# Paged attention behind a conditional mix, one core: the mixed tile is transposed by VectorE and transfers instead of TensorE, the opening is reordered and the last projection is cut into two column halves

## The chip, the cores and the metric

One core of a Trainium2 chip runs the whole program. The time is the device time of one execution in microseconds (us). Three executions of the kernel before took 2167.09, 2168.49 and 2169.05 us, so the median is 2168.49 us. Lower is better. All arithmetic is float32.

## What is computed

The input x has 64 batches of 32 tokens with 512 channels. It goes through two residual layers:

```python
# layer 1: each batch mixes its 32 tokens with one of 16 matrices
W = weights[condition]                       # 64 x 32 x 32
x = x + einsum('bct,bcd->bdt', x, W)
# layer 2: attention over 512 cached tokens (16 pages of 32) and the 32 new ones
q = rope(rmsnorm(x @ Wq.T)); k = rope(rmsnorm(x @ Wk.T)); v = x @ Wv.T   # 32 q heads, 8 k/v heads, D = 128
k_all = concat(k_cache[block_table], k); v_all = concat(v_cache[block_table], v)
p = softmax(where(valid, q @ k_all.T / sqrt(128), -1e30))
x = x + (p @ v_all) @ Wo.T
```

## The kernel before

**Tiles and steps.** The 64 batches make 16 tiles of 4 batches (128 tokens, one per partition). The 8 key heads are split into two halves of 4. The loop over steps (L949) runs first all 16 tiles with half 0, then all 16 with half 1: 32 steps. In a step the loops over 4 batches (`bt`) and 4 key heads (`g`) make 16 slots, numbered 0 to 15.

**One slot.** `scores` (L591) makes the scores of one batch and head on TensorE (`ps`), and ScalarE takes their exponential (`pr`). `values` (L647) multiplies the `pr` of the slot before with the cached values (`po`), and VectorE adds and divides. `head_keys` (L582) copies the keys of one head of the next batch out of the raw pages `k_t` into `kh` on VectorE.

**Pieces between slots.** The step also prepares the next ones. For the step after it (`ahead`, n+1): the key projection `k_a` in slot 3, the four query projections `q_a` in slots 4 to 7, and the value projection `v_a` in slot 13. All of these take the transposed tile `x1t` as weights (`project`, L420). The output projection of the step before, `out_proj` (L534), lies in slots 8 and 9. For the step after next (`beyond`, n+2) the residual tile `acc` is loaded in slot 11 (`x1_a`, L359), the mix is made in slot 14 (`x1_c`, L371: one TensorE product `pmix` with a block-diagonal matrix `bd`, then a VectorE addition), and the transposed tile is made in slot 15 (`x1_b`, L378: four TensorE transposes into `px1t`, a ScalarE copy to `x1t`, L385, and a store of `x1t` to device memory, L387 and L390, which ScalarE's queue issues). In the second half of the heads nothing is mixed: `x1_t` (L365) loads the stored `x1t` in slot 13.

**What sets the order.** TensorE and SyncE (SP) run in the order in which the program is written (L88); VectorE, ScalarE and GpSimd are ordered by a scheduler, except in the opening (L90), where all five are written out by hand. SP issues nearly all transfers, one after the other: the 16 pages of keys of each batch (L306; the pages of a batch are issued two batches ahead of its scores, and those of the batch prepared in slot 12 as 8 pages in slot 12 and 8 in slot 13, L957 and L998), the spreading of the query rows (L487), the loads and stores of `acc` (L363, L554). Transfers issued by SP and ScalarE share eight completion semaphores in turn: each transfer waits, before it is issued, until the transfer eight before it has landed. The raw pages have two buffers, `x1t` and the working tiles `w1` and `w2` one each, `acc` three.

**The opening.** The first tile's `acc` is loaded and mixed (L815) and transposed (L823) with short filler products (`keep_warm`, L803) around it. VectorE computes the rotation angles of the first two tiles (`positions`, `angles`, L819 to 821) before the transpose is asked for; ScalarE has the sines of the first angles ahead of the copy of the first `x1t`. ScalarE's queue issues the small inputs in the order condition, page table, lengths, frequencies (L747 to L793).

**The end.** After the last slot `out_proj` of the last step is done at once (L1047): 16 products of 128x512, one addition, one store. With 12 of them issued, `in_range` (L1035) lets TensorE sum a check on the denominators.

Of the kernel before, what the change touches and what calls it, by code (L numbers as in the profile page):

```python
# [55 lines left out]
def cond_resid_paged_attention_kernel(  # L56
# [69 lines left out]
    def positions():  # L126
        nc.vector.memset(half_pi, math.pi / 2)
        nc.vector.memset(minus_half, -0.5)
        nc.vector.tensor_copy(pos, lens_sb)
        nc.vector.tensor_scalar(pos, pos, row, None, ALU.add)  # L130
# [34 lines left out]
            scale=-1.0,  # L165
        )

    def cached_rows(pages_at, lens_at):

        row2 = const.tile([P, 1], F32, tag="row2", name="row2")  # L170
        nc.vector.tensor_scalar(row2, row, float(NHH), None, ALU.mult)
        nc.vector.tensor_scalar(
            v_row, pages_at, float(PSIZE * NHH), row2, ALU.mult, ALU.add
        )
        nc.vector.tensor_copy(lens_all, lens_at)
        for c in range(VC):
            key = const.tile([P, 1], F32, tag=f"key{c}", name=f"key{c}")
            nc.vector.tensor_scalar_add(key, part, float(c * P))
            nc.vector.tensor_scalar(valid[:, :, c], lens_all, key, None, ALU.is_gt)
# [15 lines left out]
    def steps_of(exact, pools):  # L195
# [130 lines left out]
        def fetch(n, c, **place):  # L326

            place = place or {"tag": "raw", "bufs": RAW}
            if c == 0 and n == NT * BT:
                other_half(1.0)  # L330
            b = n % (NT * BT)
            raw = work.tile([P, GH, D], F32, name=f"raw_{b}_{c}_{uid}", **place)
            nc.gpsimd.indirect_dma_start(  # L333
                out=raw.rearrange("p g d -> p (g d)"),
                out_offset=None,
                in_=vc,
                in_offset=bass.IndirectOffsetOnAxis(
                    ap=v_row[:, b * VC + c : b * VC + c + 1], axis=0
                ),
            )  # L340
            raws[n, c] = raw
# [22 lines left out]

        def x1_t(st):  # L365

            if st.hh:
                st.x1t = work.tile([P, KC, P], F32, tag="x1t", name=f"x1t_{st.name}", bufs=1)
                nc.sync.dma_start(st.x1t.rearrange("p c q -> p (c q)"), x1t_d[st.t])

        def x1_c(st):  # L371
            if st.hh:
                return
            pm = ps_p.tile([P, 512], F32, tag="pp", name=f"pmix_{st.name}")
            nc.tensor.matmul(pm, bd, st.acc, start=True, stop=True)  # L375
            nc.vector.tensor_tensor(st.acc, pm, st.acc, ALU.add)

        def x1_b(st):  # L378
            if st.hh:
                return  # L380
            pm = ps_p.tile([P, KC, P], F32, tag="pp", name=f"px1t_{st.name}")
            for c in range(KC):
                nc.tensor.transpose(pm[:, c, :], st.acc[:, c * P : (c + 1) * P], ident)  # L383
            st.x1t = work.tile([P, KC, P], F32, tag="x1t", name=f"x1t_{st.name}", bufs=1)
            nc.scalar.copy(st.x1t, pm)  # L385
            if st.n or exact:
                keep_x1t(st, nc.scalar)  # L387

        def keep_x1t(st, eng):
            eng.dma_start(x1t_d[st.t], st.x1t.rearrange("p c q -> p (c q)"))  # L390

        def rot_tables(st):

# [98 lines left out]
        def by_tensor(st):  # L492
            return st.n < 2 or exact
# [16 lines left out]
        def k_a(st):  # L510
            name = f"k_{st.name}"
            finish(st, GH, project(st, wt["k", st.hh, 0], f"pp_{name}"), name, "k")
# [18 lines left out]
        def q_b(st, g):  # L531
            to_columns(st, g)

        def out_proj(st, part, halfway=None):  # L534

            if part.start == 0:
                st.po = ps_p.tile([P, HID], F32, tag="pp", name=f"pout_{st.name}")
            for i in range(part.start, part.stop):
                if halfway and i == 3 * QH // 4:
                    halfway()  # L540
                nc.tensor.matmul(  # L541
                    st.po,
                    st.ot[:, i, :],
                    wt["o", st.hh, i // 4][:, i % 4, :],
                    start=(i == 0),
                    stop=(i == QH - 1),
                )
            if part.stop == QH:
                nc.vector.tensor_tensor(st.acc, st.po, st.acc, ALU.add)  # L549
                if exact or st is steps[-1]:  # L550
                    store(st)

        def store(st):
            nc.sync.dma_start(  # L554
                out[st.t * P : (st.t + 1) * P, :] if st.hh else acc_d[st.t], st.acc
            )

        def new_ot(st):
            st.ot = act.tile([P, QH, P], F32, tag="ot", name=f"ot_{st.name}", bufs=1)
# [185 lines left out]
        steps = [Step(n) for n in range(NHH * NT)]  # L745
        if not exact:
            nc.scalar.dma_start(cond_row, cond.rearrange("(i s) t -> s t i", s=S)[0:1])  # L747
            nc.scalar.dma_start(pages_sb, pages)
            nc.gpsimd.dma_start(norm_w["q"], qn_w.partition_broadcast(P))
            nc.gpsimd.dma_start(norm_w["k"], kn_w.partition_broadcast(P))  # L750
        if exact:
            nc.gpsimd.memset(vn_bufs[0], 0.0)
            nc.gpsimd.memset(vn_bufs[1], 0.0)
            key_no = wpool.tile([P, LK], F32, tag="key_no", name="key_no")
            key_no_i = work.tile([P, LK], I32, tag="sm", name="key_no_i")
            nc.gpsimd.iota(key_no_i, pattern=[[1, LK]], base=0, channel_multiplier=0)
            nc.vector.tensor_copy(key_no, key_no_i)
            nc.vector.memset(key_no[:, L:LK], -1e9)
            for st in steps:
                if st.t == 0:  # L760
                    load_w("k", st.hh)
                    load_w("v", st.hh)
                    for g in range(GH):
                        load_w("q", st.hh, g)
                        load_w("o", st.hh, g)
                if not st.hh:
                    load_cond_weights(st.t)
                x1_a(st)
                x1_t(st)
                x1_c(st)  # L770
                x1_b(st)
                rot_tables(st)
                k_a(st)
                k_b(st)
                v_a(st)
                for g in range(GH):
                    q_a(st, g)
                    q_b(st, g)
                new_ot(st)
                for bt in range(BT):  # L780
                    exact_batch(Batch(st, bt), key_no)
                out_proj(st, slice(0, QH))
            return
# [5 lines left out]
        nc.sync.dma_start(w_all, w_cond.rearrange("(n s) e -> s n e", s=S))  # L789
        load_w("q", 0, 0)  # L790
        load_w("q", 0, 1)
        nc.scalar.dma_start(lens_sb, lens)
        nc.scalar.dma_start(freq, inv_freq.partition_broadcast(P))  # L793
        load_w("k", 0, eng=nc.gpsimd)
        pages_at = work.tile([P, B * VC], I32, tag="pr", name="pages_at", bufs=3)
        nc.scalar.dma_start(pages_at, pages_v)
# [6 lines left out]
        def keep_warm(n):  # L803
            warm = ps_p.tile([P, P], F32, tag="pp", name="warm")
            for _ in range(n):
                nc.tensor.matmul(warm, ident, ident, start=True, stop=True)
# [9 lines left out]
        load_cond_weights(1)  # L816
        load_w("q", 0, 3)
        later = Batch(first, 1)
        positions()  # L819
        trig = work.tile([P, 3, TRIG * HD], F32, tag="w1", name="trig0", bufs=1)  # L820
        angles(0, trig)
        keep_warm(4)
        x1_b(first)  # L823
        keep_warm(3)
        rot_tables(first)
        nc.vector.memset(vn_bufs[0][:, :, D : D + 1], 1.0)
        nc.vector.memset(vn_bufs[1][:, :, D : D + 1], 1.0)
        cached_rows(pages_at, lens_at)
        trig = work.tile([P, 3, TRIG * HD], F32, tag="w1", name="trig1", bufs=1)
        reduced(TRIG, trig)  # L830
        q_a(first, 0)
        sines(TRIG, trig)
        early = small.tile([P, 1], F32, tag="rs", name="early")
        nc.scalar.activation(early, half_pi, AF.Exp)
        fetch(0, 0)
        fetch(0, 1)
        k_a(first)
        fetch(0, 2)
        keep_x1t(first, nc.gpsimd)
        q_a(first, 1)  # L840
# [108 lines left out]
        for st in steps:  # L949
# [3 lines left out]
            for bt in range(0 if st.n else 1, BT):  # L953
                this, after = batch, None
                n = st.n * BT + bt + 2
                if n < NHH * NT * BT:
                    after = Batch(steps[n // BT], n % BT, NPP // 2 if bt == BT - 1 else NPP)  # L957
                    unfilled += [(after, c) for c in range(VC)]
                for g in range(GH):
                    slot = bt * GH + g  # L960
# [32 lines left out]
                        if slot == 11:  # L993
                            x1_a(beyond)
                    if slot == 13:
                        if beyond:
                            x1_t(beyond)
                        for load in after.pages_left if after else ():  # L998
                            load()
                    if slot == 14 and beyond:  # L1000
                        x1_c(beyond)
                    if slot == 15 and beyond:
                        x1_b(beyond)
                    if slot == 1 and st.n == NT:
                        count(0)
                    if st.n == 1 and slot in (4, 5):
# [37 lines left out]
                redo, pc, float(P * NHH * NT * BT * GH), None, ALU.not_equal  # L1044
            )

        out_proj(steps[-1], slice(0, QH), in_range)  # L1047

    redo = const.tile([1, 1], I32, tag="redo", name="redo")
    run(False)  # L1050
# [54 lines left out]
```

## Time and profile before

The profiled execution took 2168.11 us, and its span (first to last instruction) is 2166.3 us, so 1.8 us lie outside the span.

| engine | busy us | share of the span |
|---|---|---|
| TensorE (PE) | 2144.2 | 99% |
| TensorE weight load (PEld) | 1494.4 | 69% |
| VectorE (DVE) | 1196.5 | 55% |
| ScalarE (ACT) | 868.9 | 40% |
| GpSimd (POOL) | 804.7 | 37% |

| group | count | busy us | mean ns |
|---|---|---|---|
| `po`, PE | 4096 | 551.1 | 277 |
| `pp_q`, PE | 1024 | 463.2 | 595 |
| `pout`, PE | 1024 | 450.2 | 592 |
| `pmix`, PE | 32 | 16.5 | 597 |
| `px1t`, PE | 64 | 9.7 | 273 |
| `x1t` copy, ACT | 16 | 9.3 | 581 |

A product of two float32 tiles is recorded as two passes, a transpose as one. PE products overlap, so the mean duration of one is longer than what it adds to the engine's time; the busy time counts overlaps once. "Idle before, releaser" of a group is the time its engine stood still ahead of it, and what ended most of that. For SP the timeline shows when each transfer is issued, not when it lands; a landing is seen only where something waits for it.

### The profile page before, as it was taken

What the parts mean: (1) busy time and instruction counts of PE and PEld (TensorE: products, weight loads), DVE (VectorE), ACT (ScalarE), POOL (GpSimd) and SP (SyncE); (2) the same over time, 40 slices, a digit from 0 to 9 for tenths busy, and PEclk for the clock granted to TensorE, in tenths of its full rate; (3) what the DMA queues carried; (4) which work ended last, traced back from release to release, by engine and by line L of the source; (5) the groups of instructions that cost most, each with busy time, mean ns of one, the idle gap of its engine ahead of it and who ended that gap; (6) DMA issues with size and microseconds to landing.
All of it is one profiled execution on the core that took longest, in us unless ns stands there. A gap on an engine that the chain in (4) does not pass through costs nothing.

```text
span 2166.3 us, 41552 instructions
## 1 busy us (share of the span) xinstructions
PE 2144.2 (99%) x12972; PEld 1494.4 (69%) x12972; DVE 1196.5 (55%) x2883; ACT 868.9 (40%) x1577; POOL 804.7 (37%) x1005
## 2 busy tenths in 40 slices
PE   7999999999999999999999999999999999999998
PEld 4766777667776677766777766777666777667775
DVE  5666555666455564465554565644566545556442
ACT  3544444444333344333444333443334443334441
POOL 4433333433333343333433343433434333334330
PEclk9999999999999999999999999999999999999999
DMA  8765555555655556556766855565545565555551
GB/s 248 193 164 162 157 172 157 148 155 160 172 152 152 151 160 174 154 150 196 224 177 179 212 158 164 157 178 159 156 141 169 162 174 159 153 153 163 171 162 54
DMA packets 387638, 357.51 MB, mean 165 GB/s; under 512 B 55024, under 2 KB 317296, under 8 KB 387408
## 3 DMA queue, kind: packets, MB, share of 16 engines
q1 hardware_dynamic: 342864, 213.87, 35.1%
q0 software_dynamic: 41648, 136.74, 21.6%
q10 hardware_dynamic: 2896, 4.14, 0.5%
q8 instruction: 106, 1.74, 0.3%
q14 instruction: 124, 1.02, 0.2%
HBM read 302.64 MB, written 12.58 MB: 146 GB/s over the span
## 4 chain that ended last, share of the span: by engine, by line
PE 97%; ACT 0%; issue 0%; DVE 0%
PE po_x L653 22%; PE ps_x L595 21%; PE pout_x L541 20%; PE pp_q_x L423 20%; PE pp_k_x L423 5%; PE pp_v_x L423 5%; PE pnv_x L637 2%; PE psn_x L613 1%; PE pmix_x L375 1%; PE px1t_x L383 0%; PE pt_x L467 0%; ACT pr_x L603 0%; ACT v_x L346 0%; DVE acc_x L549 0%; ACT nv_x L645 0%
## 5 line engine op out<-in xcount | busy, mean ns | idle before, releaser
L333 POOL DMA_INDIRECT raw_x<-in_vc_dram,v_row x512 | 540.4, 1055 | 820.4 <-ACT v_x L346 752.0
L603 ACT ACTIVATE pr_x<-ps_x 128x512 f32<-128x512 f32 x512 | 305.9, 597 | 825.5 <-PE ps_x L595 756.8
L653 PEld LDWEIGHTS po_x<-v_x,pr_x 128*128 128x128 f32 x4096 | 515.7, 192 | 126.9 <-issue 114.5
L653 PE MATMUL po_x<-v_x,pr_x 128*128 128x129 f32 x4096 | 551.1, 277 | 2.3 <-ACT pr_x L603 1.6
L423 PE MATMUL pp_q_x<-wq_x,x1t_x 128*128 128x512 f32 x1024 | 463.2, 595 | 8.5 <-ACT x1t_x L385 8.2
L541 PE MATMUL pout_x<-wo_x,ot_x 128*128 128x512 f32 x1024 | 450.2, 592 | 0.0
L595 PE MATMUL ps_x<-q_cols_x,kh_x 128*128 128x128 f32 x3072 | 405.4, 275 | 0.0
L595 PEld LDWEIGHTS ps_x<-q_cols_x,kh_x 128*128 128x128 f32 x3072 | 376.1, 192 | 15.1 <-issue 14.6
L346 ACT ACTIVATE v_x<-raw_x,valid 128x512 f32<-128x512 f32 x512 | 363.0, 716 | 5.3 <-DMA raw_x<-in_vc_dram,v_row 5.1
L541 PEld LDWEIGHTS pout_x<-wo_x,ot_x 128*128 128x128 f32 x1024 | 189.7, 190 | 214.3 <-issue 214.0
L423 PEld LDWEIGHTS pp_q_x<-wq_x,x1t_x 128*128 128x128 f32 x1024 | 185.8, 191 | 194.4 <-issue 185.6
L588 DVE COPY kh_x<-k_t_x 128x512 f32<-128x512 f32 x506 | 206.0, 417 | 188.1 <-PE ps_x L595 153.8
L671 DVE TENSOR_TENSOR nv_x<-po_x,nv_x 128x258 f32<-128x258 f32 x256 | 108.4, 424 | 314.9 <-PE po_x L653 279.9
L440 POOL TENSOR_TENSOR rs_q_x<-ms_q_x,minus_half 128x4 f32<-128x4 f32 x128 | 140.8, 1100 | 170.1 <-DVE ms_q_x L438 169.9
L433 ACT ACTIVATE sq_q_x<-pp_q_x 128x512 f32<-128x512 f32 x128 | 76.6, 598 | 272.9 <-PE pp_q_x L423 178.9
L595 PE MATMUL ps_x<-q_last_x,kh_x 128*128 128x128 f32 x1024 | 135.2, 275 | 0.0
L549 DVE TENSOR_TENSOR acc_x<-pout_x,acc_x 128x512 f32<-128x512 f32 x32 | 22.1, 692 | 199.3 <-PE pout_x L541 199.3
L595 PEld LDWEIGHTS ps_x<-q_last_x,kh_x 128*128 128x128 f32 x1024 | 124.6, 192 | 0.0
L423 PE MATMUL pp_k_x<-wk_x,x1t_x 128*128 128x512 f32 x256 | 116.3, 597 | 0.9 <-ACT x1t_x L385 0.9
L423 PE MATMUL pp_v_x<-wv_x,x1t_x 128*128 128x512 f32 x256 | 115.2, 592 | 0.0
L674 DVE TENSOR_TENSOR o_x<-nv_x,rden 128x256 f32<-128x256 f32 x256 | 108.6, 424 | 6.2
L437 DVE TENSOR_REDUCE ms_q_x<-sq_q_x 128x4 f32<-128x512 f32 x128 | 86.5, 676 | 45.1 <-ACT sq_q_x L433 44.6
(105 smaller groups left out, 1455.1 us busy)
## 6 DMA issues: line engine op xcount, KB each, us to landing
k_t_x<-in_kt_dram SPq DMA_DIRECT2D x2048, 64.0 KB
q_cols_x<-rows_x SPq DMA_DIRECT2D x360, 80.0 KB
q_last_x<-rows_x SPq DMA_DIRECT2D x120, 80.0 KB
raw_x<-in_vc_dram,v_row POOLq DMA_INDIRECT x512
wo_x<-in_wo_dram SPq DMA_DIRECT2D x32, 256.0 KB
acc_x<-in_x_dram SPq DMA_DIRECT2D x16, 256.0 KB
acc_d<-acc_x SPq DMA_DIRECT2D x16, 256.0 KB
wq_x<-in_wq_dram SPq DMA_DIRECT2D x8, 512.0 KB
```

Source lines behind the costliest of these rows:

```text
L333: nc.gpsimd.indirect_dma_start(out=raw.rearrange("p g d -> p (g d)"), out_offset=None, in_=vc, in_offset=bass.IndirectOffsetOnAxis(ap=v_ro ...
L346: nc.scalar.activation(v_bufs[b % 2][:, c, :, 0:D], raw, AF.Copy, scale=ok)
L423: nc.tensor.matmul(pp, st.x1t[:, c, :], w[:, c, :], start=(c == 0), stop=(c == KC - 1))
L437: nc.vector.tensor_reduce(ms, sq, AX.X, ALU.add)
L440: nc.gpsimd.tensor_tensor(rs, ms, minus_half, ALU.pow)
L541: nc.tensor.matmul(st.po, st.ot[:, i, :], wt["o", st.hh, i // 4][:, i % 4, :], start=(i == 0), stop=(i == QH - 1),)
L588: last["dve"] = nc.vector.tensor_copy(k, ba.k_raw[:, :, g, :]).ins
L595: nc.tensor.matmul(ps[:, c, :], ba.k[g][:, c * P : (c + 1) * P], queries(ba, g), start=True, stop=True,)
L603: last["act"] = nc.scalar.activation(pr, ps, AF.Exp, scale=SCALE).ins
L653: nc.tensor.matmul(ba.po[:, g % 2, :], ba.pr[g][:, c, :], ba.v_t[:, c, g, :], start=(c == 0), stop=(c == VC - 1),)
L671: nc.vector.tensor_tensor(t, ba.po, t, ALU.add)
L674: nc.vector.tensor_tensor(ba.o[:, both, :], t[:, :, 0:D], rd.unsqueeze(2).to_broadcast([P, 2, D]), ALU.mult,)
```

## The change

1. `x1_b` takes a new way for the tiles of steps 2 to 15 (14 tiles), `x1_turn`. VectorE transposes the mixed tile in blocks of 32x32 into a `w1` tile, and SP issues four transfers, one per batch, that store the blocks in device memory at the places of the full transpose, in runs of 32 floats (128 bytes). TensorE's transposes, ScalarE's copy and ScalarE's store are gone for these tiles. The first two tiles keep them.
2. The mix (`x1_c`) and `x1_turn` both move to slot 13, behind `v_a` and ahead of the last 8 pages that slot 13 issues.
3. The stored tile is loaded into `x1t` (`x1_t`) at the beginning of the next step: after the first 4 of the 16 pages that are issued there (`back`), and the other 12 pages follow.
4. Opening: the first `x1t` is asked for ahead of the angles; ScalarE's copy goes ahead of the sines; frequencies and lengths are issued ahead of the page table; `cached_rows` is cut in two, the row numbers come after the first query projection and the masks (`looked_at`) after the first key projection.
5. The last projection is made in two halves of 256 columns, each with its own addition and store; the check on the denominators lies in the first.

```diff
         def x1_t(st):
-            if st.hh:
-                st.x1t = work.tile([P, KC, P], F32, tag="x1t", name=f"x1t_{st.name}", bufs=1)
-                nc.sync.dma_start(st.x1t.rearrange("p c q -> p (c q)"), x1t_d[st.t])
+            st.x1t = work.tile([P, KC, P], F32, tag="x1t", name=f"x1t_{st.name}", bufs=1)
+            nc.sync.dma_start(st.x1t.rearrange("p c q -> p (c q)"), x1t_d[st.t])
...
         def x1_b(st):
             if st.hh:
                 return
+            if not by_tensor(st):
+                return x1_turn(st)
...
+        def x1_turn(st):
+            turned = work.tile([P, KC * BT, S], F32, tag="w1", name=f"x1w_{st.name}", bufs=1)
+            nc.vector.transpose(turned, st.acc.rearrange("p (j d) -> p j d", d=S))
+            kept = x1t_d[st.t].rearrange("(j d) (c b x) -> b d c j x", d=S, b=BT, x=S)
+            for b in range(BT):
+                nc.sync.dma_start(
+                    kept[b],
+                    turned[b * S : (b + 1) * S, :, :].rearrange("p (c j) x -> p c j x", c=KC),
+                )
...
+                back = bt == 0 and ahead and not ahead.hh
                 if n < NHH * NT * BT:
-                    after = Batch(steps[n // BT], n % BT, NPP // 2 if bt == BT - 1 else NPP)
+                    after = Batch(
+                        steps[n // BT],
+                        n % BT,
+                        NPP // 4 if back else NPP // 2 if bt == BT - 1 else NPP,
+                    )
+                    if back:
+                        x1_t(ahead)
+                        for load in after.pages_left:
+                            load()
...
                     if slot == 13:
-                        if beyond:
+                        if beyond and beyond.hh:
                             x1_t(beyond)
+                        elif beyond:
+                            x1_c(beyond)
+                            x1_b(beyond)
                         for load in after.pages_left if after else ():
                             load()
-                    if slot == 14 and beyond:
-                        x1_c(beyond)
-                    if slot == 15 and beyond:
-                        x1_b(beyond)
...
+            nc.scalar.dma_start(freq, inv_freq.partition_broadcast(P))
+            nc.scalar.dma_start(lens_sb, lens)
             nc.scalar.dma_start(pages_sb, pages)
...
-        nc.scalar.dma_start(lens_sb, lens)
-        nc.scalar.dma_start(freq, inv_freq.partition_broadcast(P))
...
+        keep_warm(4)
+        x1_b(first)
+        keep_warm(3)
         positions()
         trig = work.tile([P, 3, TRIG * HD], F32, tag="w1", name="trig0", bufs=1)
         angles(0, trig)
-        keep_warm(4)
-        x1_b(first)
-        keep_warm(3)
         rot_tables(first)
...
-        cached_rows(pages_at, lens_at)
...
+        cached_rows(pages_at)
         fetch(0, 0)
         fetch(0, 1)
         k_a(first)
+        looked_at(lens_at)
...
-        out_proj(steps[-1], slice(0, QH), in_range)
+        out_proj(steps[-1], slice(0, QH), slice(0, HID // 2), in_range)
+        out_proj(steps[-1], slice(0, QH), slice(HID // 2, HID))
```

More of the change, by code (lines that the diff above doesn't have):

```diff
@@ L166, in sines, with cached_rows @@
         )
-    def cached_rows(pages_at, lens_at):
+    def cached_rows(pages_at):
         row2 = const.tile([P, 1], F32, tag="row2", name="row2")
@@ L174, in cached_rows, with looked_at @@
         )
+    def looked_at(lens_at):
         nc.vector.tensor_copy(lens_all, lens_at)
@@ L532, in q_b, with out_proj @@
             to_columns(st, g)
-        def out_proj(st, part, halfway=None):
-            if part.start == 0:
+        def out_proj(st, part, cols=slice(0, HID), halfway=None):
+            if part.start == 0 and cols.start == 0:
                 st.po = ps_p.tile([P, HID], F32, tag="pp", name=f"pout_{st.name}")
@@ L541, in out_proj @@
                 nc.tensor.matmul(
-                    st.po,
+                    st.po[:, cols],
                     st.ot[:, i, :],
-                    wt["o", st.hh, i // 4][:, i % 4, :],
+                    wt["o", st.hh, i // 4][:, i % 4, cols],
                     start=(i == 0),
@@ L548, in out_proj, with store @@
             if part.stop == QH:
-                nc.vector.tensor_tensor(st.acc, st.po, st.acc, ALU.add)
+                nc.vector.tensor_tensor(st.acc[:, cols], st.po[:, cols], st.acc[:, cols], ALU.add)
                 if exact or st is steps[-1]:
[L551 to L556, printed above, removed]
+                    store(st, cols)
+        def store(st, cols=slice(0, HID)):
+            dst = out[st.t * P : (st.t + 1) * P, :] if st.hh else acc_d[st.t]
+            nc.sync.dma_start(dst[:, cols], st.acc[:, cols])
         def new_ot(st):
@@ L768, in steps_of @@
                 x1_a(st)
-                x1_t(st)
+                if st.hh:
+                    x1_t(st)
                 x1_c(st)
```

## Prediction

> **What bounds the kernel now.** I read the page first, its busy times and its chain of work that ended last.
>
> ```profile
> PE 2144.2 (99%) x12972; PEld 1494.4 (69%) x12972; DVE 1196.5 (55%) x2883; ACT 868.9 (40%) x1577; POOL 804.7 (37%) x1005
> ...
> PE 97%; ACT 0%; issue 0%; DVE 0%
> ```
>
> TensorE bounds it: of 2166.3 us only 22 are without a product. So a product taken off TensorE is a gain, and every new wait of TensorE is a loss in full. Who made it wait tells the list of its waits:
>
> ```profile
> PE pp_q_x L423 <- ACT x1t_x L385: 8.2, 1, 8.2
> PE po_x L653 <- ACT pr_x L603: 1.6, 1, 1.6
> PE warm L806 <- POOL ident masks.py:199: 1.6, 1, 1.6
> PE pp_k_x L423 <- ACT x1t_x L385: 0.9, 1, 0.9
> ```
>
> The one long wait is in the opening, for the first `x1t`. In the steps TensorE waits for nothing, so all that is fed to it has slack, and the slack is what the change spends. The chain in order of time, around the end of one step (start, us, what), gives the true price of each piece:
>
> ```profile
> 434.07 0.86 PE pmix_x L375 x2
> ...
> 436.71 0.44 PE px1t_x L383 x4
> ...
> 448.10 1.29 PE pp_k_x L423 x3
> ```
>
> Four transposes add 0.44 us. The distance between output projections confirms it: 67.15 us per step in the first half (204.79 to 943.39 in 11 steps), 65.88 in the second (1142.32 to 1998.78 in 13), and 1.27 is about 0.86 + 0.44. Last, the timeline of SP in the same stretch, and of one store of `x1t`:
>
> ```profile
> 428.00 0.53 SPq L363 DMA_DIRECT2D acc_x<-in_x_dram  x1
> ...
> 433.56 0.33 SPq L306 DMA_DIRECT2D k_t_x<-in_kt_dram  x1
> ...
> 438.28 0.33 SPq L306 DMA_DIRECT2D k_t_x<-in_kt_dram  x1
> 441.34 0.33 SPq L306 DMA_DIRECT2D k_t_x<-in_kt_dram  x1
> ```
> ```profile
> 505.04 0.33 ACTq L390 DMA_DIRECT2D x1t_d<-x1t_x  x1
> ```
> ```profile
> 510.04 0.33 SPq L306 DMA_DIRECT2D k_t_x<-in_kt_dram  x1
> ```
>
> SP is busy without a pause from slot 11 into the next step, one page every 0.52 us; between two batches it loads page numbers, 2.4 to 2.7 us in the steps I looked at. The page at 510.04 waited for the semaphore of the store of 505.04: 256 KB landed 5.0 us after issue. Others took 4.9, 4.2 and at most 3.3.
>
> [...] The change stores pieces of 128 bytes; nothing in this trace does. [...] granted clock 0.50 from 12 us on, after idling from 8.7.
>
> **The change, part by part.**
>
> *Transposes off TensorE.* 14 x 0.44 = 6.2 us gained. Moving `pmix` changes nothing by itself, unless `acc` is late: it was needed at 433.91 and is now at 432.12, and was issued at 428.00. From the bytes moved after 428 I put its landing near 431.3, so 0; if it lands later, up to 0.5 x 14 = 7 us of loss.
>
> *ScalarE* loses a copy of 0.58 us and a store issue of 0.33 per tile. It is 40% busy and TensorE doesn't wait for it in the steps: 0. *VectorE* gains a 0.71 us transpose per tile at 55% load; the addition runs next to it in a place where it idled 4.07 us: 0. If that cover went, 14 x 0.71 = 10 us.
>
> *The way through memory.* This is the step that decides. I lay it on the step above, taking the old times until `pmix`.
> - `pmix` starts at 432.12, behind `pp_v`. The addition begins 1.06 later (433.91 to 434.97), takes 0.69, the transpose 0.7: the first store is ready at 434.6. SP has its first 8 pages out by 434, so nothing queues ahead.
> - Four store issues, 0.55 each as in the spreads: until 436.8.
> - Then the last 8 pages of slot 13. The first four go out by 438.9; the last four have the semaphores of the four stores, and wait until these land. The data: 4 x 512 pieces = 128 per engine. The only row with such pieces is the load of `w_all`: between 3.4 and 3.6 us the engines spent 2.4 us on 69 of them, 34 ns each; between 4.0 and 4.2, 24 ns. With 30 ns, 3.8 us, and 0.7 for one gather of 256 KB beside them (at 384 GB/s). They begin about 1.2 us after the first issue, so data end at 440.3; [...] (the 256 KB stores leave 1.4 to 3.1 after start and data) the fourth has landed at 442.3.
> - Last page out at 442.7, page numbers 2.5, four pages 2.1: the load of `x1t` is issued at 447.3.
> - It lands 3.5 us later (`acc`, as large, about 3.3; a wait on such a load ended at most 4.7 after issue): 450.8.
> - `pp_k` wants it at 447.94 - 0.44 = 447.5. TensorE stands still for 3.3 us; behind it in its order are the scores of slot 4 and all query projections.
>
> 14 readbacks x 3.3 = 46 us lost. Bounds: with no semaphore wait and the shortest of each, the load is out at 445.2 and lands at 448.5, 1.0 us per step, 14 us; if page numbers take the 1.3 seen at another batch boundary, 0 or an early arrival. [...] I take 3.3.
>
> The 4 stores and the load also delay pages: about 2.6 us plus the waits. Keys of the batch prepared in slot 12 were copied from 442.83 on and are wanted by scores at 451.38, so 8 us cover it: 0; without them the delay of 3 to 5 us would fall on TensorE. The move of the load away from slot 13 concerns only the first half; the second keeps it.
>
> *Opening.* The wait of 8.2 us loses its reason: ScalarE no longer has three sines ahead of the copy, which can end near 8.9 instead of 16.9. What is late next is the first query weight, 1 MB. By 10 us 1.76 MB had moved, about 0.5 of it small inputs; two queues share the rest, so some 0.63 MB of this weight was there; the other 0.42 at half of 384 GB/s comes by 12.2[...]. Gain 16.96 - 12.8 = 4.2. The page table, now third on ScalarE's queue, may land at 13.4 (where the third landed) instead of 8.6; its pages lost 6 us to semaphores anyway (16 took 14.7 us, not 8.3), so their end hardly moves. Value, second `acc`, last query weight and later pages follow on SP as before, with up to 5 us of slack (keys of the second batch were there at 48.9, scores at 55.2). I take 4.0; between 0 (weights late) and 8.2 + 2.4 (also the clock: the first projection took 6.05 us instead of 3.6).
>
> *Last projection.* 32 passes of 512 columns at 0.43 become 64 of 256 at half. The last addition shrinks from 0.69 to 0.43 (row of 258 columns), the store by half: 0.4 gained; between -0.3 (pass overhead) and 0.8.
>
> *Sum.* -6.2 - 4.0 - 0.4 + 46 = +35.6. On the profiled execution, 2168.1 (span 2166.3 and 1.8 outside), 2203.7; the median, 2168.5, is 0.4 higher: **2204**.
>
> **Rivals.**
> *The readback is in time, so it is faster.* For it: SP's pieces each have shorter examples (1.3 for page numbers, 0.47 for an issue of 512 pieces in the opening), and the load is placed after only four pages. Against: these would all have to be short at once, to save 3.3 us. Then 2168.5 - 6.2 - 4.0 - 0.4 = 2158. It decides at 10.6 / 14 = 0.76 us of stall per step: below, faster; above, slower. Around it, within 0.2% (4.3 us, what a measurement of this kernel can tell from no change), the stall is 0.45 to 1.06.
> *The stores drain much more slowly, and the clock falls.* [...] With 7 us of stall and 0.5 of clock: 2168.5 - 10.6 + 14 x 7.5 = 2263. Against: the engines handle 128 byte reads in 24 to 34 ns.
>
> **How the numbers follow.** Stall of 1.1 to 5.5 per step (2173 to 2235): 0.58, likeliest, 2204. Slow stores: 0.19. Balance, within 0.2%: 0.06. In time, faster: 0.17. So faster 0.17, same 0.06, slower 0.77. The range, 2157 to 2250, leaves out the half of the faster case with a larger opening gain, and the upper two thirds of the slow stores, together 0.2. Likeliest case alone: 2173 to 2235.
>
> **What would show it.** Right: `pp_k` waits for the load of `x1t`, 14 times, about 3 us each; SP waits before the last pages of slot 13 for the stores; first-half steps of about 70 us, second-half ones at 65.9; the first query projection starts near 13. Wrong: no such wait and steps of 66.7, or a wait of `pmix` for `acc`, or VectorE late with the transpose, or an opening still tied to page table or keys.

## The result, and the profile after

After the change the median is 2207.4 us (four runs, 2200.3 to 2212.0) against 2168.8 before: the ratio is 1.0177, 95% interval 1.0165 to 1.0190, so 38 us slower. The profiled execution took 2203.99 us, its span is 2202.2: 35.9 more than the span before. The four runs are spread over 12 us, those of before over 2.3.

The page, busy times and chain of work that ended last:

```profile
PE 2152.6 (98%) x12948; PEld 1498.0 (68%) x12948; DVE 1206.4 (55%) x2898; ACT 863.0 (39%) x1564; POOL 802.3 (36%) x1005
...
PE 89%; SPq 4%; DMA 3%; issue 1%; DVE 1%; ACT 0%; DVEq 0%; ACTq 0%
```

TensorE has 56 transposes fewer and 32 passes of the halved last projection more, and yet is busy 8.4 us longer, so some products have become slower; and it stands still 49.6 us instead of 22.1. SyncE (SPq) and transfers, which the chain of before did not have at all, now hold 7% of it. The list of TensorE's waits (total, times, longest) names the places:

```profile
PE pp_k_x L439 <- DMA x1t_x<-x1t_d: 26.2, 14, 3.1
PE pp_v_x L439 <- DMA wv_x<-in_wv_dram: 4.3, 1, 4.3
PE pp_q_x L439 <- DMA wq_x<-in_wq_dram: 3.2, 2, 2.3
PE pmix_x L377 <- DMA k_t_x<-in_kt_dram: 2.0, 2, 1.0
...
PE pmix_x L377 <- DMA acc_x<-in_x_dram: 1.1, 1, 1.1
```

Fourteen waits for the readback of `x1t` are there, one in each of the fourteen steps that need it, as forecast. The wait of 8.2 us for the first `x1t` is gone; in its place stand waits for weights. And the mix, which never waited before, waits about 1 us three times. What becomes slower is seen in the group of key projections, before and after:

```profile
L423 PE MATMUL pp_k_x<-wk_x,x1t_x 128*128 128x512 f32 x256 | 116.3, 597 | 0.9 <-ACT x1t_x L385 0.9
```
```profile
L439 PE MATMUL pp_k_x<-wk_x,x1t_x 128*128 128x512 f32 x256 | 125.0, 634 | 27.2 <-DMA x1t_x<-x1t_d 26.2
```

The mean of one product rises from 597 to 634 ns, and the group's busy time, in which overlaps count once, by 8.7 us. It isn't spread over the fourteen steps: four of them, behind waits of 2.56, 3.11, 2.96 and 2.63, have eight products of 5.2 to 6.5 us instead of 3.6, and in just these four stretches of the steps the granted clock is 0.50. The other ten take 3.67. Two of the four in the timeline:

```profile
116.76 5.37 PE L439 MATMUL pp_k_x<-wk_x,x1t_x 128*128 128x512 f32 x8 [2.56 <-DMA x1t_x<-x1t_d]
...
189.86 6.47 PE L439 MATMUL pp_k_x<-wk_x,x1t_x 128*128 128x512 f32 x8 [3.11 <-DMA x1t_x<-x1t_d]
```

Last, one way through memory from end to end, the chain in order of time at the end of step 5 (start, us, what). It is the stretch that the prediction worked out:

```profile
454.69 1.11 PE pmix_x L377 x2
455.83 0.70 DVE acc_x L378
...
456.62 0.72 DVE x1w_x L400
457.36 0.64 SPq L403
...
458.05 0.62 SPq L403
...
458.73 0.62 SPq L403
...
459.39 0.63 SPq L403
...
460.20 0.48 SPq L309
...
464.08 0.31 SPq L309
...
464.43 1.02 SPq L301
...
465.70 0.33 SPq L309
...
466.74 1.32 SPq L309
...
468.67 2.73 DMA x1t_x<-x1t_d
471.41 0.14 issue
471.54 3.67 PE pp_k_x L439 x8
```

There is no hole in it: mix, addition, transpose, four stores 0.67 apart (predicted 0.55), eight pages in 4.2, the page numbers in 1.02 (1.3 from the last page to the first of the next batch), four pages in 3.0 (one of them 1.32; in seven of the 14 steps they take 2.0 to 2.1), and the readback lands 2.7 us after its issue. From the first store to the readback's issue it is 11.3 here, 10.7 to 12.4 over the 14 steps with a mean of 11.5; the prediction had 12.7. The wait for the stores' semaphores, which it put before the last four pages, isn't there in this step: page five follows store one by 5.1 us, page eight store four by 4.7, and neither waits, so the stores have landed by then. In eight of the other steps one or two of the eight pages took 0.8 to 2.2 us to issue. The list of SyncE's waits names none of these stores, and in four of the eight steps it is a page ahead of the fifth, which has no store's semaphore; in the rest a wait for a store isn't ruled out. SyncE also stands still ahead of the first store: it waits 13 times for VectorE's transpose, 12.3 us in all.

### The profile page after: what moved, and what is told of

It is laid out like the page before. It is cut to its first block, busy times and chain, and to the rows that moved or that the text cites. A ratio compares the mean times of both kernels' runs of the same rounds, so it can differ in the third digit from the quotient of the medians.

```text
span 2202.2 us, 41677 instructions
## 1 busy us (share of the span) xinstructions
PE 2152.6 (98%) x12948; PEld 1498.0 (68%) x12948; DVE 1206.4 (55%) x2898; ACT 863.0 (39%) x1564; POOL 802.3 (36%) x1005
## 3 DMA queue, kind: packets, MB, share of 16 engines
q14 instruction: 126, 1.02, 0.2%
## 4 chain that ended last, share of the span: by engine, by line
PE 89%; SPq 4%; DMA 3%; issue 1%; DVE 1%; ACT 0%; DVEq 0%; ACTq 0%
PE pout_x L557 20%; PE pp_q_x L439 19%; PE po_x L668 18%; PE ps_x L610 18%; PE pp_k_x L439 5%; PE pp_v_x L439 4%; SPq L309 2%; DMA x1t_x<-x1t_d 2%; PE pnv_x L652 1%; PE psn_x L628 1%; SPq L403 1%; PE pmix_x L377 1%; SPq L301 0%; SPq L503 0%; DMA acc_x<-in_x_dram 0%
## 5 line engine op out<-in xcount | busy, mean ns | idle before, releaser
L557 PE MATMUL pout_x<-wo_x,ot_x 128*128 128x512 f32 (+1 forms) x1056 | 450.5, 580 | 0.5 <-DVE acc_x L565 0.5
L557 PEld LDWEIGHTS pout_x<-wo_x,ot_x 128*128 128x128 f32 x1056 | 195.7, 190 | 210.0 <-issue 207.3
L439 PE MATMUL pp_k_x<-wk_x,x1t_x 128*128 128x512 f32 x256 | 125.0, 634 | 27.2 <-DMA x1t_x<-x1t_d 26.2
L565 DVE TENSOR_TENSOR acc_x<-pout_x,acc_x 128x512 f32<-128x512 f32 (+1 forms) x33 | 22.3, 676 | 204.9 <-PE pout_x L557 204.9
L453 DVE TENSOR_REDUCE ms_k_x<-sq_k_x 128x4 f32<-128x512 f32 x32 | 21.9, 686 | 164.6 <-ACT sq_k_x L449 164.6
```

Source lines behind the costliest of these rows:

```text
L439: nc.tensor.matmul(pp, st.x1t[:, c, :], w[:, c, :], start=(c == 0), stop=(c == KC - 1))
L557: nc.tensor.matmul(st.po[:, cols], st.ot[:, i, :], wt["o", st.hh, i // 4][:, i % 4, cols], start=(i == 0), stop=(i == QH - 1),)
```

## The experiments

My theory after this trace: the loss is the readback's place on SyncE. SyncE issues one transfer after another (a page every 0.52 us, a store every 0.67), and what it issues ahead of the readback sets the wait; the slow clock adds to it; the opening lost its gain. The rivals: the stores land late, the mix and VectorE, the readback's landing itself. All ratios are to the kernel before, run on the same chip as the experiment.

**1. The opening alone.** The kernel before with the diff's edits to the opening and to `cached_rows`, nothing else.

> The kernel before with the changed kernel's opening alone: transposes of the first tile and the warm-up products ahead of positions and angles, the frequencies' and lengths' transfers ahead of the page numbers, the cache rows and the lengths split and later. Step of the prediction that this tries: the opening gives 4.0 us (so 2164.8). My theory after reading the changed trace: TensorE starts its first projection 4.6 us sooner, then waits 4.3 us for the first value weights, whose load stands on SyncE's queue behind the first batch's pages, and the pages wait for the page numbers, which now come after two more transfers; the projection after that wait starts at the old time and at the slow clock. So +1.9 us: 2170.7, first value projection at 34.9 us from the start as before with a wait of about 4 us ahead of it. Rival: the wait for the value weights comes from something of the rest of the change, then 2164 to 2166.

Measured: 1.0011 (1.0004 to 1.0018), +2.4 us, where the prediction had -4.0. The 21 runs spread over 7.4 us, those of before over 4.7. TensorE starts the first projection at 12.37 instead of 16.96, waits 1.65 us for the first keys and 1.75 for the value weights, and runs the value projection in 5.37 instead of 3.6. In the median the gain doesn't exist, and the loss belongs to the opening itself.

In single executions it does exist. Runs 2, 3, 4 and 7 below have the same opening, and the second mix, which follows the first value projection, starts in their traces at 35.35, 37.13, 36.41 and 35.62: 1.7 to 3.4 us sooner than in the trace of before. In run 1 it starts at 39.12, in the changed kernel at 40.65. Before the change, and in run 2:

```profile
38.79 1.02 PE L375 MATMUL pmix_x<-acc_x,bd 128*128 128x512 f32 x2
```
```profile
31.42 3.66 PE L439 MATMUL pp_v_x<-wv_x,x1t_x 128*128 128x512 f32 x8
...
35.35 1.02 PE L377 MATMUL pmix_x<-acc_x,bd 128*128 128x512 f32 x2
```

SyncE issued the value weights between 24.61 and 25.72 in all six traces. The waits for them were 0 to 2.63 us in the four, and the projection took 3.67 at the most; only in the other two was it slow, 5.37 in run 1 and 5.43 in the changed kernel, there at a granted clock of 0.50. The 21 executions of run 1 say that the loss is the usual outcome. What makes the weights late in one execution and not in the next wasn't tried.

**2 and 3. The readback's place.**

```diff
-                        NPP // 4 if back else NPP // 2 if bt == BT - 1 else NPP,
+                        0 if back else NPP // 2 if bt == BT - 1 else NPP,         (2)
+                        NPP // 2 if back else NPP // 2 if bt == BT - 1 else NPP,  (3)
```

> The changed kernel with the readback of the mixed input issued ahead of every page of the next batch instead of after four of its sixteen. My theory: the chain from the mix to the key projection is bound by what SyncE issues one after the other; four pages fewer ahead of the readback take 4 x 0.52 = 2.1 us off the wait in each of 14 steps. Of waits of 1.0 to 3.1 us (about 30 in all) some 4 us stay, and the restarts at the slow clock (about 8.6 us in all) mostly go: 2207 - 26 to - 35, so 2172 to 2181. Rival, as the prediction had it: the four stores land late and a readback issued sooner waits for them instead; then the gain is under 0.7 us a step, 2198 to 2207. Rival two: the loss is not in the readback at all (the mix at slot 13, VectorE's transposes): 2207.

> The changed kernel with the readback issued after eight pages of the next batch instead of four. My theory (SyncE's issues one after the other): 4 x 0.52 = 2.1 us more wait in each of 14 steps = +29, and with waits of 3 to 5 us the projection behind each restarts at the slow clock, at 1.8 to 2.7 us for the some ten steps that do not yet: +18 to +27 more; so 2236 to 2263. Rival, loss from the mix or VectorE: 2207. Rival, the readback's landing time rather than its place: 2207 to 2212.

Measured: with no page ahead 1.0000 (0.9992 to 1.0009), all of the loss gone; with eight 1.0403 (1.0387 to 1.0419), 2252.9 us. The group of key projections with eight pages:

```profile
L439 PE MATMUL pp_k_x<-wk_x,x1t_x 128*128 128x512 f32 x256 | 145.2, 720 | 56.6 <-DMA x1t_x<-x1t_d 55.7
```

The waits grew from 26.2 to 55.7: 29.5 / 14 = 2.1 us a step, which is four pages at 0.52, as expected. The mean product went to 720 ns: all fourteen projections ran slow, and the group is busy 28.9 us longer than before. With no page ahead 0.2 us of waiting for the readback is left, or 1.2 with one wait of 1.04 that the profile puts down to ScalarE and that ended 2.8 us after the readback's issue. That is more gain than I had expected (2172 to 2181 against 2167.5): the readback's issue came 8.8 us after the first store on average instead of 11.5, so the four pages with what they waited for had been worth 2.7 us, not 2.1.

**4. One store in place of four.**

```diff
-            for b in range(BT):
-                nc.sync.dma_start(kept[b], turned[b * S : (b + 1) * S, :, :]...)
+            nc.sync.dma_start(x1t_d[st.t], turned.rearrange("p j x -> p (j x)"))
```

> The changed kernel with one plain store of VectorE's 32x32 transposes in place of four stores that put the blocks in their places. It leaves out the placing of blocks, so the projections of 14 tiles work on blocks in a wrong order; all sizes and the rest of the work are as they were. My theory (SyncE's issues): three stores of 0.67 us fewer ahead of the readback, 2.0 us off each of 14 waits, so like the readback ahead of the pages: 2172 to 2182. Rival: what counts is the mix and the transposes ahead of the stores, or the landing of the readback: 2200 to 2207.

It leaves out the placing of the blocks. Measured: 1.0003 (0.9995 to 1.0012), 2166.8 us; waits for the readback fell to 0.8 us in two steps. Pages ahead of it and stores ahead of it are worth the same: what counts is how much SyncE issues, whichever it is. One plain store may also land sooner than four scattered ones, so this run alone would not tell issue from landing; with the second and the third, and no store in SyncE's list of waits, the issues are the better supported of the two. It also came out better than expected.

**5. Value weights ahead of the pages.** As the first, and `load_w("v", 0)` moved above `batch = Batch(first, 0)`.

> The kernel before with the changed kernel's opening, and in it the load of the first value weights ahead of the first batch's pages on SyncE's queue instead of behind them. My theory: the opening lost its gain to those weights standing behind pages that wait for the page numbers; ahead of them they land in the stretch from 20 to 25 us in which the DMA engines are half idle, and the first value projection waits no more: the prediction's 4.0 us are gained, 2163.0 against the 2167.0 of before (2162 to 2165). Rival: the transfers of the opening are bound by what the DMA engines move; the weights then push the third query weights and the pages back by the 3 us that their megabyte takes, and the time is 2166 to 2170.

Measured: 1.0009 (1.0001 to 1.0017): nothing is mended, and the time is the rival's. The wait moved to the first scores:

```profile
32.88 2.07 PE L598 MATMUL ps_x<-q_cols_x,kh_x 128*128 128x128 f32 x8 [4.06 <-ACT kh_x L589]
34.74 4.33 PE L426 MATMUL pp_v_x<-wv_x,x1t_x 128*128 128x512 f32 x8
```

The keys of the first batch are late now, and the value projection begins at 34.74, where it was before (34.92). Moving one load ahead of the other gains nothing.

**6. The mix at slot 13 alone.** In the kernel before, `x1_c(beyond)` from slot 14 to slot 13, ahead of the pages; the transposes stay.

> The kernel before with the mix in slot 13, right after the value projection and ahead of the pages, as the changed kernel has it; TensorE's transposes stay in slot 15, nothing goes through memory. The prediction put this move at 0 with a bound of +7. My theory: the tile's input is loaded in slot 11 behind four stores, and lands about when slot 13's mix wants it; with the readback out of the way 5 of 14 mixes waited 0.2 to 0.9 us, and mixes do not wait at slot 14: +2.5, 2169.5 (2168.5 to 2171). Rival: the input is in time when nothing else has moved: 2167.0. Rival two: TensorE's order around the mix costs a wait in each step: up to +7, 2174.

Measured: 1.0009 (1.0003 to 1.0016), +1.9 us. The move that the prediction took at 0 costs about what the trace after had suggested. But its own trace shows only one wait of the mix for `acc`, 0.29 us, and two of 0.06; thirteen steps of the first half are 1.0 us longer in all than before. That the late `acc` is the whole of the 1.9 isn't shown.

**7. Spare products during the wait.**

```diff
+            if name.startswith("pp_k") and st.n > 1 and not st.hh and not exact:
+                for _ in range(4):
+                    nc.tensor.matmul(pp[:, 0:P], ident, ident, start=True, stop=True)
```

> The changed kernel with four spare products of 128 by 128 ahead of the key projection in each of the 14 steps, written to the projection's own accumulator before it begins (they change no output). They need nothing from the readback, take 0.5 to 1.1 us, and so cut TensorE's longest idle stretch from 3.1 to some 2.3 us. My theory: some 30 of the change's 41 us are the wait itself, which stays, and about 8.6 are the projections that run at the slow clock after it; those go: 2198 to 2201. Rival: the slow projections are chance that idle length does not set: 2205 to 2212.

Measured: 1.0140 (1.0122 to 1.0158), 2193.0 us; the changed kernel had 1.0177 (1.0165 to 1.0190). The difference, 0.0037, is 8 us, about what I expected for the slow products (8.6):

```profile
L442 PE MATMUL pp_k_x<-wk_x,x1t_x 128*128 128x512 f32 x256 | 116.6, 598 | 11.1 <-DMA x1t_x<-x1t_d 10.0
```

With work that nobody needs (14 times 1.06 us) the real products are back at 598 ns. The rest of the wait, 10.0 us and the spare products' 14.8, still stands. In this trace the granted clock never falls between the opening and the end, and its mean is 0.997, as in the trace before; in the changed kernel it was 0.994. So the slow products came with TensorE's idling in these waits, and with part of it filled they were gone.

**8, 9, 10. Versions without the wait.** 8: the readback ahead of the pages, the value weights as in 5, and in slot 11 `x1_a(beyond)` ahead of the four stores of the query rows instead of behind them. 9: the same with the whole opening of before. 10: as 9, with the changed opening, but the page numbers' transfer ahead of the frequencies and lengths on ScalarE's queue, as before.

> The changed kernel with the readback ahead of the next batch's pages, the first value weights ahead of the first batch's pages, and in slot 11 the tile's input loaded ahead of the four stores instead of behind them. My theory: transposes -6.2, opening -4.0, last projection -0.7, mix no longer late: 2167.0 - 10.9 = 2156 (2155 to 2161). Rival: the input's load now waits for the store that frees its buffer and holds the four stores behind it, so the mix stays late and the next batch's scores wait too: 2160 to 2168.

> The kernel of the run before with the opening of the kernel before the change: readback ahead of the next batch's pages, tile's input ahead of the four stores in slot 11, everything ahead of the main loop as it was. My theory now: the opening is bound by its transfers whatever TensorE does in it, and the changed opening costs about 2 us because the wait that moved in front of the value projection makes a second start at the slow clock; without it the steps give -6.2 (14 transposes) and the end -0.7: 6.9 below before, that is 0.9968 of it, and about 2 to 3 below the run with the changed opening. Rival: the changed opening's slowness came from something that the first value weights' place already mended; then this equals the run before, 0.998 of the kernel before.

> The same with the changed opening except for one thing: the page numbers' transfer stays ahead of the frequencies' and lengths', as before the change, so that SyncE begins the first batch's pages at 10.0 us instead of 13.9. The value weights stand behind the pages as in the changed kernel. Theory one (order of transfers): pages and value weights are then in time for a TensorE that started 4.6 us sooner, and the prediction's 4.0 us appear: 0.9968 - 0.0018 = 0.995 of the kernel before. Theory two (the amount of transfers): SyncE's issues of the pages are held back by the weights still under way, so the last page and the value weights land where they did, the wait stays in front of the value projection: 0.997 to 0.998.

Measured: 0.9982 (0.9974 to 0.9991), 0.9976 (0.9967 to 0.9985), 0.9986 (0.9979 to 0.9993). All three beat both kernels, the ninth by 5.2 us, with runs that spread over 2.1 us; eight and ten, with the changed opening, spread over 9 and 14. In the eighth and the ninth no mix waits; steps of the first half take mostly 66.7 us, against 67.13 before: that is the 0.44 of the transposes, undisturbed. The ninth is 1.7 us slower than my sum of -6.2 - 0.7; its interval overlaps the eighth's, so these two alone don't show the old opening to be the better. The eighth's 2160.71 lies in the expected 2155 to 2161 only because that chip ran the kernel before in 2164.86; as a ratio 0.9945 to 0.9972 was expected, and what is missing is the gain of the opening. The tenth began the pages at 10.6 us, and it did not help (start, us, what):

```profile
10.60 15.18 SPq L309 DMA_DIRECT2D k_t_x<-in_kt_dram  x16
25.83 0.42 SPq L262 DMA_DIRECT2D wv_x<-in_wv_dram  x1
```
```profile
33.65 5.37 PE L439 MATMUL pp_v_x<-wv_x,x1t_x 128*128 128x512 f32 x8 [3.12 <-DMA wv_x<-in_wv_dram]
```

Sixteen pages took 15.2 us to issue; the longest of SyncE's waits among them, 3.1 us, was for query weights on their way. Neither order gives the opening its gain in the median.

**11. Less to move in the opening; 12. spare products in it.** Both on the first run's kernel.

```diff
-        load_w("q", 0, 2, eng=nc.gpsimd)
+        wt["q", 0, 2] = wpool.tile([P, 4, 512], F32, tag="wq2", ...)
+        nc.gpsimd.tensor_copy(wt["q", 0, 2], wt["q", 0, 0])    (11)
...
+        keep_warm(6)                                          (12)
         new = v_product(first)
```

> The kernel before with the changed opening alone, as in the first of these runs, but the third query weights (1 MB) are not loaded: GpSimd copies the first ones in their place, so a quarter of the queries of the first half use wrong weights; everything else is as it was. Theory: the wait in front of the first value projection is set by the amount that must be moved ahead of its weights. 1 MB less at the 384 GB/s of that stretch is 2.7 us, so the value weights land by about 31 us, the wait of 1.7 us or more goes, and with it the slow start of 1.8: 3 to 4 us under the changed opening alone, 0.9993 to 0.9998 of the kernel before where that was 1.0011. Rival: what counts is when SyncE issues the weights, behind pages that wait for page numbers: 1.001, as the changed opening alone.

> The kernel before with the changed opening alone, and six spare products of 128 by 128 (some 1.7 us) ahead of the first value projection, where TensorE waits for its weights; they change no output. Theory: the wait stays, but the projection behind it starts at full clock, which saves up to 1.8 us where the wait was long, and costs up to 1.7 where there was no wait: 1.0002 to 1.0011 of the kernel before, against 1.0011 for the changed opening alone. If the second start at the slow clock is not what makes the changed opening slower than the old one, nothing is saved: 1.0011 to 1.0015.

The eleventh leaves out the third query weights. Measured: 0.9984 (0.9978 to 0.9991) and 1.0003 (0.9996 to 1.0011). With one of the megabytes not moved:

```profile
13.70 8.14 SPq L309 DMA_DIRECT2D k_t_x<-in_kt_dram  x16
21.90 0.43 SPq L262 DMA_DIRECT2D wv_x<-in_wv_dram  x1
```
```profile
29.38 3.60 PE L426 MATMUL pp_v_x<-wv_x,x1t_x 128*128 128x512 f32 x8
```

The pages begin as late as in the changed kernel, at 13.7, but go out at 0.51 us each, and the value projection starts 4.1 us sooner than in run 1 and 5.6 sooner than in the changed kernel, without a wait and at full speed. The prediction's gain appears, 3.5 us, as soon as a megabyte less is to be moved, and that is more than I expected (0.9993 to 0.9998). The amount ahead matters, then, where the order didn't. But it isn't only the amount: SyncE also issues the value weights 3.3 us sooner than in run 1 (21.90 against 25.22), and between 20 and 26 us of run 1 the DMA engines are 31, 41 and 70% busy, so there they don't bind. This run doesn't part fewer bytes from an earlier issue. The twelfth is 1.7 us under the first run by the ratios, as the slow second start would have it, but the intervals overlap: likely, not shown.

## Why the prediction was right, and where its steps were not

The predicted 2204 lies 3 us under the measured median, and the profiled execution, 2203.99, agrees with the 2203.7 that the sum gave. Part of this is luck: the main step was right in kind and too large, and three smaller ones were missed on the other side.

| step | predicted, us | in the profile after, us |
|---|---|---|
| transposes off TensorE | -6.2 | -6.2 (0.44 a step in run 8) |
| waits for the readback | +46.2 | +26.2 |
| slow products behind these waits | in a rival only | +8.7 |
| mix in slot 13 | 0, bound 7 | +3.2 (run 6: +1.9) |
| opening | -4.0 | +1.9 in this execution (run 1: +2.4) |
| last projection | -0.4 | -0.7 |
| not assigned |  | +2.8 |
| sum | +35.6 | +35.9 |

*Transposes, ScalarE, VectorE.* Right. Between the opening and the last projection of the changed kernel the two hold TensorE up for 0.3 us; after the addition VectorE transposes in 0.72 without a gap.

*The way through memory.* Right: the readback is the step that decides, it comes too late in every step, SyncE's issues make it so, and TensorE pays: 1.9 us a step on average instead of 3.3. The balance point of 0.76 us a step was too high: runs 2 and 4, with almost no wait left, should by it be some 10 us faster than before, and are level, because the opening and the mix keep the gain away. Too large was the term for the stores: I had the fourth land 7.7 us after the first could go out, of which the last 2 were my estimate, and the last of the eight pages wait for it. In the step shown that page goes out 6.7 us after the first store and waits for nothing; the stores were down within 4.7 to 5.1 us of their issue. From the last page to the next batch's first it took 1.3, not 2.5. In the other direction store issues took 0.67 instead of 0.55, and the four pages 3.0 instead of 2.1. SyncE's readbacks of 256 KB landed in 2.7 to 4.1; the prediction had 3.5. For the stores in pieces of 128 bytes no wait is on SyncE's list, and what such a store costs the DMA engines wasn't measured.

*The clock.* The prediction had read a granted clock of 0.50 behind the one long idle stretch of the trace before, 8.2 us in the opening, and put a slow clock in the steps only into the rival with an assumed 7 us of wait. In the trace after, it was 0.50 behind four waits of 2.56 to 3.11 us as well, and the slow products there were 8.7 of the 35.9 us.

*Mix.* The bound was right and the value was not: `acc` was estimated to land 0.8 us before the mix wants it, and that was less than it varies: in the trace after the mix waited about 1 us in three steps and 0.1 or less in the others. The profile puts one of the three down to `acc` and two to pages, but in each the last record of `acc`'s own semaphore falls 0.04 to 0.13 us before the mix starts, 5.0 to 5.4 us after `acc`'s issue; the prediction had 3.3.

*Opening.* This is the step that failed, in the median in sign: "Value, second `acc`, last query weight and later pages follow on SP as before, with up to 5 us of slack". They follow as before, and that is the trouble: the value weights were issued at 25.00 and before the change at 24.74, and TensorE, 4.6 us sooner through its first projections, used up the slack and waited 4.28:

```profile
34.94 5.43 PE L439 MATMUL pp_v_x<-wv_x,x1t_x 128*128 128x512 f32 x8 [4.28 <-DMA wv_x<-in_wv_dram]
```
```profile
34.92 3.60 PE L423 MATMUL pp_v_x<-wv_x,x1t_x 128*128 128x512 f32 x8
```

The start is the same to 0.02 us, the projection 1.83 longer, and this is the opening's +1.9. It was priced by the first wait alone; when the next weights land, with all that is ahead of them, was worked out for the first query weights and not for the value weights. That the outcome changes from one execution to the next (a gain of 1.7 to 3.4 in the traces of runs 2, 3, 4 and 7) was not foreseen either. The landing of the first query weights at 12.8 was in part my estimate; the first query projection started at 12.35.

*Last projection.* The second half's products wait 0.5 us for the first half's addition, and still 0.7 is gained.

*Rivals.* "In time" named the right thing to change: four pages fewer and it is in time, but it ends level, not at 2158. The ninth run, with the mix mended and the old opening, is at 2161.7. "Slow stores and the clock" had the wrong cause; the third run, 2252.9, comes near its 2263, where eight pages do what the stores did not. The 7 us of stall behind the 2263 were my assumption.

What stays open: 2.8 us of the account, why the ninth run gained 1.7 us less than its sum (its first-half steps are longer than 66.69 us by 1.1 in all), and what decides the opening from one execution to the next.

## What to carry to other kernels

When a tile goes out to memory and comes back, write down everything that the issuing queue sends between the store and the load, page numbers included, at its measured pitch; then ask which of it may stand behind the load. Four issues were worth the whole measured loss here. When a wait is removed early in a kernel, follow the consumer to its next transfer and compare when that lands with when it will now be wanted; if that landing hasn't moved, the wait only moves: here it became 4.28 us ahead of the value weights' projection, which then took 5.43 us instead of 3.60, at a granted clock of 0.50.

## What the hardware showed that I had not expected

- In the changed kernel TensorE's eight products behind waits of 2.56, 2.63, 2.96 and 3.11 us took 5.37, 5.37, 5.19 and 6.47 us instead of 3.6, with a granted clock of 0.50 in part or all of that time. The wait's length alone doesn't sort them: behind waits of 2.47 and 2.78 they took 3.67, and in run 3 they took 5.37 behind 2.21. What does was not shown. In run 7, with spare products in the wait (longest idle stretch 2.0), it happened in none of 14 steps. Two stretches of the changed kernel, one within the products behind the wait of 2.56 and one from the middle of those behind 2.47 on (stretch, its length and TensorE's busy time; the third number from the end is the clock):

```profile
117.00:120.40 3.40, 3.40 (x5) 1.36 (x5) 0.00 (x0) 0.00 (x0) 0.00 (x0) 0.50 0.70 201
...
263.77:267.17 3.40, 3.40 (x15) 2.03 (x14) 0.72 (x2) 1.00 (x2) 0.00 (x0) 1.00 0.55 162
```

- A store of 64 KB in 512 pieces of 128 bytes took SyncE 0.67 us from one issue to the next, a page of 64 KB 0.52.
- Readbacks of 256 KB landed 2.7 to 4.1 us after issue in the changed kernel; in run 2 one took 4.96 and cost 0.2 us of waiting, in run 4 one took 5.5 and cost 0.5.
- The kernels with the changed opening spread more from execution to execution: 7.4 to 14 us in runs 1, 5, 8 and 10, though only 5.3 and 5.8 in runs 11 and 12; with the old opening it is 2.1 in run 9, 5.7 in run 6 and 3.0 to 5.2 in three of the four sets of runs of the kernel before (9.5 in the fourth).
